# The layer norm's residual of a two-layer scan network: added by GpSimd, or by an accumulating DMA; norm and features centred in place

## The chip, the cores and the metric

The kernel runs on one core of a Trainium2 chip. A core has a matrix engine (PE, with its weight loads PEld), a vector engine (DVE), an activation engine (ACT), a general engine (POOL, or GpSimd) and a queue engine that only issues DMAs (SP). Each works through its own queue in order and waits for semaphores of the others. The metric is the device time of one execution in microseconds (us); the median of three runs is used.

## The reference, cut to what matters

The input x is 2 x 256 x 64 x 64, taken as 2 batches of 4096 tokens of 256 channels. Layer 0 is a group norm and one selective state-space scan. Layer 1 normalises each token, adds a forward and a backward scan of a second normalisation of it, and then a mixture of eight experts:

```python
x = x + _L0_conv_ref(_gn(x), ...)
t = _to_tokens(x)
t = t + _L1_attn_ref(_ln_t(t), ...)
t = t + _L1_ffn_ref(_ln_t(t), ...)

def _core(x, ln_gamma, ln_beta, fp, bp):       # called by _L1_attn_ref with x = _ln_t(t)
    xn = (x - mu) / jnp.sqrt(var + 1e-05) * ln_gamma + ln_beta
    y_fwd = _mamba(xn, *fp)
    y_bwd = jnp.flip(_mamba(jnp.flip(xn, 1), *bp), 1)
    return y_fwd + y_bwd + x
```

So layer 1's stream becomes t + ln(t) + y_fwd + y_bwd, where ln(t) is the norm before it is normalised again. The sum t + ln(t) is what the change touches. Everything is float32.

## The kernel before, in words

**Tiles and jobs.** A chunk is 512 tokens (T); a tile of the stream is 128 partitions x 2 halves of the channels x 512 (512 KB). Each batch has three jobs: layer 0 (256 inner channels, nj = 2), the forward scan of layer 1 (512, nj = 4) and the flipped one (nj = 4). A job does its 8 chunks in order; a chunk of a job is a *step* i, 48 in all. The stream t lives in DRAM (`t_dram`, one tensor per batch).

**The scan.** A step consists of nj x 4 *quads*. For a quad, POOL makes bq = rxdt x bc (line 737, 128x2048), ACT two halves of the decays da (line 747, into PSUM), DVE scans each half (line 773) and multiplies with C (line 782); for three quads of eight, and one half quad of sixteen, POOL does that multiplication (line 798). PE sums over the states (line 806). ACT also adds the carried state to the first element of bq (line 758) ahead of a half quad's decays.

**Order.** A *slot* is half a quad; step i starts at slot `starts[i]`, a forward or flipped step has 32 slots and one of layer 0 has 16. Everything beside the scan is put by hand at a slot and a queue with `sl.put(slot, queue, fn)`, relative to the start s0 of its step, and `in_order()` fixes each engine's queue in that order. In a slot, ACT first makes the decays of the next slot and then what was put there; DVE scans, then does what was put; POOL does its quads and then what was put. Matrix products of the experts fill free places: `experts()` chooses slots from counts of products, activations and PSUM banks that each part has registered with `sl.count`.

**The norm of a forward step** (`norm`): at slot -48 SP loads x from `t_dram` (line 370); PE takes the mean (line 389); DVE centres x into a tile cen (line 395); ACT squares (line 399); PE takes the variance (line 404); ACT makes the roots; DVE divides into nx (line 414), which is ln(t), and scales cen for the second normalisation (line 415), both at slot -39 (late is 1 slot more in batch 0). At the same slot POOL adds x and nx (line 418). At -35 ACT writes gamma and beta's result over nx (line 422; -38 for the first chunk), and at -34 SP stores nx for the flipped job (line 428) and x back to `t_dram` (line 429). For the first chunk of a job all is 6 slots later.

**The end of a step** (`finish`): SP loads the stream into xr (line 829) 10 slots before the end of a forward or flipped step; PE projects the gated scan and adds xr (lines 836, 838) at 16 and 18 slots after the end (7 and 8 in layer 0); ACT copies the result back into xr (line 853); SP stores it to `t_dram` two slots after the second projection (line 854). For a flipped step `features` then makes the normalised features that the experts read: mean, centring by DVE into a tile fcen one slot after that store (line 871), square (line 876), variance, division (line 886) and a store to `nf_dram` (line 891). Tiles x, xr, and cen with fcen have one buffer each; nx has two.

**The last stage** (from line 1141) does the remaining experts and the gate, and is no part of the change.

Of the kernel before, what the change touches and what calls it, by code (L numbers as in the profile page):

```python
# [42 lines left out]
F32 = mybir.dt.float32  # L43
AF = mybir.ActivationFunctionType
ALU = mybir.AluOpType
AX = mybir.AxisListType

P = 128
NB, C, L = 2, 256, 4096
KC = C // P  # L50
T = 512
NCH = L // T
# [19 lines left out]
SLOTS = {  # L72
    2: dict(xs=(-23, -22), conv=(-20,), dbc=-16, dt=(-14, -13), z=(-10, -9), out=(7, 8)),
    4: dict(
        xs=(-31, -30, -24, -23), conv=(-26, -21), dbc=-17, dt=(-15, -13, -11, -9), z=(-6, -5, -3, -2),
        out=(16, 18),
    ),
}
AHEAD = 3
# [55 lines left out]
def hybrid_kernel(ctx: ExitStack, tc: tile.TileContext, a: dict, out: bass.AP):  # L135
    nc = tc.nc
# [32 lines left out]
    t_dram = [drp.tile([P, KC, L], F32, name=f"t_dram{b}") for b in range(NB)]  # L169
# [12 lines left out]
    def rsqrt(dst, src, eps, scale=1.0):  # L182
        nc.scalar.activation(dst, src, AF.Ln, bias=eps, scale=scale)
        nc.scalar.activation(dst, dst, AF.Exp, scale=-0.5)

    def over_channels(t):
        return t.rearrange("p (o t) -> p o t", o=1).to_broadcast([P, KC, T])


    with ExitStack() as st:  # L190
        wp = st.enter_context(tc.tile_pool(name="wp", bufs=1))
        wk = st.enter_context(tc.tile_pool(name="wk", bufs=1))
# [20 lines left out]
        sl = Slots()  # L213
# [130 lines left out]
        steps = [(job, c) for job in jobs for c in range(NCH)]  # L344
        starts = [sum(8 * job.nj for job, _ in steps[:i]) for i in range(len(steps) + 1)]
# [3 lines left out]
        def norm(i):  # L349

            (job, c), ck, tag, s0 = steps[i], cks[i], tags[i], starts[i]
            s = job.cols(c)
            b = job.batch
            if job is jobs[AHEAD]:
                return

            def alloc():
                ck["nx"] = wk.tile([P, KC, T], F32, tag="nx", name=f"nx_{tag}", bufs=2)

            if job.flip:  # L360
                def load():
                    alloc()
                    nc.sync.dma_start(ck["nx"], n2_dram[b][:, NCH - 1 - c, :, :])
                sl.put(s0 - 44, "sp", load)
                return

            def load_x():
                ck["x"] = wk.tile([P, KC, T], F32, tag="x", name=f"x_{tag}")
                src = t_dram[b] if job.layer else a["x"][b].rearrange("(k p) l -> p k l", p=P)
                nc.sync.dma_start(ck["x"], src[:, :, s])  # L370

            if job.layer == 0:
                def scale():
                    alloc()
                    for k in range(KC):
                        nc.scalar.activation(
                            ck["nx"][:, k, :], ck["x"][:, k, :], AF.Identity,
                            bias=job.gb[:, k : k + 1], scale=job.gs[:, k : k + 1],
                        )
                sl.put(s0 - 32, "sp", load_x)  # L380
                sl.put(s0 - 25, "act", scale)
                return

            def mean():
                ck["ps"] = psp.tile([P, T], F32, tag="ps", name=f"mean_{tag}")
                for k in range(KC):
                    nc.tensor.matmul(
                        ck["ps"], mean_w, ck["x"][:, k, :], start=(k == 0), stop=(k == KC - 1)  # L390
                    )

            def centre():
                ck["cen"] = wk.tile([P, KC, T], F32, tag="cen", name=f"cen_{tag}")
                nc.vector.tensor_tensor(ck["cen"], ck["x"], over_channels(ck["ps"]), ALU.subtract)

            def square():
                alloc()
                nc.scalar.activation(ck["nx"], ck["cen"], AF.Square)

            def variance():
                ck["var"] = psp.tile([P, T], F32, tag="ps", name=f"var_{tag}")
                for k in range(KC):
                    nc.tensor.matmul(
                        ck["var"], mean_w, ck["nx"][:, k, :], start=(k == 0), stop=(k == KC - 1)
                    )

            def roots():
                ck["r1"] = psp.tile([P, T], F32, tag="ps", name=f"r1_{tag}")
                rsqrt(ck["r1"], ck["var"], eps5)  # L410
                rsqrt(ck["var"], ck["var"], eps10, scale=1.0 + 1e-5)

            def divide():
                nc.vector.tensor_tensor(ck["nx"], ck["cen"], over_channels(ck["r1"]), ALU.mult)  # L414
                nc.vector.tensor_tensor(ck["cen"], ck["cen"], over_channels(ck["var"]), ALU.mult)

            def add():
                nc.gpsimd.tensor_tensor(ck["x"], ck["x"], ck["nx"], ALU.add)

            def affine():  # L420
                for k in range(KC):
                    nc.scalar.activation(
                        ck["nx"][:, k, :], ck["cen"][:, k, :], AF.Identity,
                        bias=lngb[:, 1, k : k + 1], scale=lngb[:, 0, k : k + 1],
                    )

            def store():
                nc.sync.dma_start(n2_dram[b][:, c, :, :], ck["nx"])
                nc.sync.dma_start(t_dram[b][:, :, s], ck["x"])

            late = 1 if NCH < i < 2 * NCH else 0
            for d, queue, fn in (
                (-48, "sp", load_x), (-44, "pe", mean), (-43, "dve", centre), (-42, "act", square),
                (late - 41, "pe", variance), (late - 40, "act", roots), (late - 39, "dve", divide), (late - 39, "pool", add),
                (-35 if c else -38, "act", affine), (-34, "sp", store),
            ):

                sl.put(s0 + d + (6 if c == 0 else 0), queue, fn)
            s0 += 6 if c == 0 else 0
            sl.count(s0 - 44, 2, 0, (1,))  # L440
            sl.count(s0 - 43, 0, 1)
            sl.count(s0 - 41, 2, 4, (2,))
            sl.count(s0 - 40, 0, 0, (1,))
            sl.count(s0 - (36 if c else 39), 0, 2.3)
# [376 lines left out]
        def finish(i):  # L821
            (job, c), ck, tag = steps[i], cks[i], tags[i]
            s, b = job.cols(c), job.batch
            v = {}

            def load():
                v["x"] = wk.tile([P, KC, T], F32, tag="xr", name=f"xr_{tag}")
                src = t_dram[b] if job.layer else a["x"][b].rearrange("(k p) l -> p k l", p=P)
                nc.sync.dma_start(v["x"], src[:, :, s])

            def over_time(m):
                return v["x"][:, m, ::-1] if job.flip else v["x"][:, m, :]

            def project(m):
                v[m] = psp.tile([P, T], F32, tag="ps", name=f"o_{tag}_{m}")
                nc.tensor.matmul(v[m], ident, over_time(m), start=True, stop=False)
                for j in range(job.nj):
                    nc.tensor.matmul(  # L838
                        v[m], job.w["out"][:, j, m * P : (m + 1) * P], ck["sz", j],
                        start=False, stop=(j == job.nj - 1),  # L840
                    )

            s0 = starts[i + 1]

            before = steps[i - 1][0].nj if i else 0
            sl.put(max(s0 - (10 if job.nj == 4 else 5), starts[i] + (21 if before == 4 else 0)), "sp", load)

            slots = SLOTS[job.nj]["out"] if i + 1 < len(steps) else (3, 4)
            for slot in slots:
                sl.count(s0 + slot, 1 + job.nj, 1, (1,))  # L850
            for m, slot in enumerate(slots):
                sl.put(s0 + slot, "pe", lambda m=m: project(m))
                sl.put(s0 + slot + 1, "act", lambda m=m: nc.scalar.copy(over_time(m), v[m]))
            sl.put(s0 + slot + 2, "sp", lambda: nc.sync.dma_start(t_dram[b][:, :, s], v["x"]))
            if job.flip and i + 1 < len(steps):
                features(b, NCH - 1 - c, v, s0 + slot + 2)

        def features(b, c, v, s0):
# [8 lines left out]
                    )  # L867

            def centre():
                v["cen"] = wk.tile([P, KC, T], F32, tag="cen", name=f"fcen_{b}{c}")  # L870
                nc.vector.tensor_tensor(v["cen"], v["x"], over_channels(v["ps"]), ALU.subtract)

            def square():
# [217 lines left out]
        for g in range(nq):  # L1091
            i, jp, n = quads[g]
# [47 lines left out]
    with ExitStack() as st:  # L1140
# [5 lines left out]
        n, x, y, acc, wts, wb, lt, w_dram = {}, {}, {}, {}, {}, {}, {}, {}  # L1146
# [329 lines left out]
```

## Time and profile before

| | |
|---|---|
| median of 3 runs | 5069.14 us (5067.45 to 5076.32) |
| the profiled execution | 5072.22 us, its span 5070.5 us |
| busy, share of the span | PE 84%, DVE 90%, ACT 71%, POOL 87% |
| scan stage | first scan at 61.6 us, last one at 4475.2 us |
| add of line 418 on POOL | 16 times, 2.36 us (median) |
| line 737 on POOL | 640 times, 4.54 us |
| line 773 on DVE | scans of 128x1024, 2.34 us each |
| DMA | 873 MB, 172 GB/s over the span |

How to read it: the page of one profiled execution gives busy times and the span in 40 slices, as tenths; lines are named by engine, line, operation, out<-in and shape, with the number of instances. The view by windows gives the busy time of each engine between two times. The view of waits lists who waited for whom (total, times, longest, in us). In the timeline a line gives start and length in us, and in brackets the idle time of the engine just before and what ended it. "DMA to landing" is the time from an issue until its semaphore tells that the data have arrived.

### The profile page before, as it was taken

To read this page: it belongs to the slowest core of one execution; us is meant where nothing else is said; L and a number is where in the kernel's file an instruction comes from. 1 tells how busy PE (TensorE), PEld (TensorE's weight loads), DVE (VectorE), ACT (ScalarE), POOL (GpSimd) and SP (SyncE) were. 2 spreads that over 40 slices of the span, in tenths; PEclk is the share of its full clock that TensorE was granted. 3 is DMA by queue.
4 is the path that set the end of the run, shared out by engine and by line. 5 is a ranking of instruction groups with operands and counts; after the bars stand their busy time and mean duration, and the time that the engine had idled before them with its cause. 6 is when DMAs were issued, how large, how long until landed. Compare 5 with 4: busy or idle time off the path is not lost. (4 is left out here: it accounts for less than half of the span.)

```text
span 5070.5 us, 47370 instructions
## 1 busy us (share of the span) xinstructions
PE 4247.6 (84%) x14920; PEld 1478.8 (29%) x14920; DVE 4581.4 (90%) x3096; ACT 3609.1 (71%) x7319; POOL 4409.8 (87%) x1442
## 2 busy tenths in 40 slices
PE   5667787787777899989999888898868999888997
PEld 1222222222222333333333333333222333334443
DVE  6998999999999999999999999999999999946635
ACT  5677777777776877877787888878777788742231
POOL 5998999999999999999999999999999999931110
PEclk8788889899888999999999999999889999999998
DMA  5455444444444444457675555544444554544533
GB/s 189 155 172 180 160 159 160 146 155 155 170 167 155 162 171 165 160 198 246 233 243 185 175 184 178 188 161 172 140 160 167 175 177 158 175 168 175 199 112 137
DMA packets 333947, 873.15 MB, mean 172 GB/s; under 512 B 36408, under 2 KB 111936, under 8 KB 291712
## 3 DMA queue, kind: packets, MB, share of 16 engines
q1 hardware_dynamic: 329408, 842.73, 48.4%
q0 software_dynamic: 4288, 27.40, 1.4%
q8 instruction: 118, 1.93, 0.2%
q14 instruction: 133, 1.09, 0.1%
HBM read 671.17 MB, written 198.84 MB: 172 GB/s over the span
## 5 line engine op out<-in xcount | busy, mean ns | idle before, releaser
L737 POOL TENSOR_TENSOR bq<-rxdt,bc 128x2048 f32<-128x2048 f32 x640 | 2892.7, 4541 | 17.3 <-DMA rxdt<-xdtd 8.3
L747 ACT ACTIVATE da<-rdt,w_a 128x512 f32<-128x512 f32 x2560 | 1757.3, 686 | 110.3 <-DVE bq L773 63.9
L773 DVE TENSOR_TENSOR_SCAN da<-da,h_state,bq 128x1024 f32<-128x1024 f32 x664 | 1558.0, 2346 | 55.3 <-ACT da L747 44.7
L798 POOL TENSOR_TENSOR bq<-bq,bc 128x2048 f32<-128x2048 f32 (+1 forms) x280 | 1180.0, 4214 | 22.5
L773 DVE TENSOR_TENSOR_SCAN bq<-da,h_state,bq 128x1024 f32<-128x1024 f32 x456 | 1059.5, 2339 | 23.7 <-ACT da L747 23.7
L806 PE MATMUL y<-bq,stack 128*32 128x512 f32 x5120 | 741.9, 665 | 275.3 <-POOL bq L798 251.5
L782 DVE TENSOR_TENSOR bq<-da,bc 128x1024 f32<-128x1024 f32 x760 | 926.3, 1219 | 15.7
L989 PE MATMUL e<-eh,ew 128*128 128x512 f32 x1376 | 671.6, 622 | 63.9 <-DMA ew<-in_Wo 17.0
L792 ACT COPY h_state<-da 128x2 f32<-128x2 f32 x759 | 119.3, 157 | 634.1 <-DVE bq L782 632.3
L758 ACT ACTIVATE bq<-h_state,bq,a 128x1 f32<-128x1 f32 x1120 | 430.2, 384 | 2.7 <-POOL bq L737 2.0
L989 PEld LDWEIGHTS e<-eh,ew 128*128 128x128 f32 x1376 | 250.7, 194 | 475.9 <-issue 239.9
L806 PEld LDWEIGHTS y<-bq,stack 128*32 128x32 f32 x5120 | 140.1, 116 | 820.2 <-POOL bq L798 359.7
L450 PE MATMUL z<-nx,w_in 128*128 128x512 f32 x640 | 329.1, 643 | 58.1 <-DVE nx L414 21.2
L523 PE MATMUL conv<-xs,w_conv 64*64 64x512 f32 x2560 | 330.1, 602 | 23.5 <-ACT xs L507 21.3
L989 PE MATMUL e<-en,ew 128*128 128x512 f32 x688 | 323.8, 604 | 22.9 <-DVE fcen L886 15.8
L450 PE MATMUL xs<-nx,w_in 128*128 128x512 f32 x640 | 317.3, 625 | 21.1 <-DVE xc L536 7.9
L1287 ACT ACTIVATE h<-hp,of,sc 128x512 f32<-128x512 f32 x168 | 130.4, 777 | 252.2 <-PE hp L1283 235.6
L838 PE MATMUL o<-sz,w_out 128*128 128x512 f32 x640 | 298.3, 605 | 0.0
L1000 ACT ACTIVATE eh<-e,of,sc 128x512 f32<-128x512 f32 x344 | 259.3, 767 | 44.1 <-PE e L989 43.9
L590 POOL TENSOR_TENSOR xdt<-sp,xc 128x512 f32<-128x512 f32 x160 | 203.3, 1275 | 46.0 <-DVE sp L586 45.8
L773 DVE TENSOR_TENSOR_SCAN da<-da,bq 128x1024 f32<-128x1024 f32 x96 | 219.4, 2285 | 3.8 <-ACT da L747 2.2
L1248 POOL TENSOR_TENSOR x<-x,bi 128x1024 f32<-128x1024 f32 x16 | 37.2, 2338 | 188.8 <-DMA x<-t_dram 108.0
(141 smaller groups left out, 4924.1 us busy)
## 6 DMA issues: line engine op xcount, KB each, us to landing
rxdt<-xdtd SPq DMA_DIRECT2D x160, 1024.0 KB, 6.6
rdt<-dtd SPq DMA_DIRECT2D x160, 1024.0 KB, 6.5
bc<-bcd SPq DMA_DIRECT2D x384, 256.0 KB, 3.2
ew<-in_W SPq DMA_DIRECT2D x172, 256.0 KB, 5.0
u<-u SPq DMA_DIRECT2D x86, 512.0 KB, 4.3
u<-eu SPq DMA_DIRECT2D x82, 512.0 KB, 4.3
dtd<-sp SPq DMA_DIRECT2D x160, 256.0 KB, 3.5
xdtd<-xdt SPq DMA_DIRECT2D x160, 256.0 KB, 3.4
```

Of the source, the lines that this page charges most:

```text
L450: nc.tensor.matmul(ps, job.matrices["in", half][:, k, j * P : (j + 1) * P], rhs, start=(k == 0), stop=(k == KC - 1),)
L523: nc.tensor.matmul(v[r][64 * col : 64 * col + 64, :], job.matrices["conv"][rows, 2 * jp + j, k, :], ck["xs", jp][rows, j, k : k + T] if k ...
L737: nc.gpsimd.tensor_tensor(bq[g], ck["rxdt", j], over_groups(ck["bc", 0, sg]), ALU.mult)
L747: nc.scalar.activation(da[g, h][:, k, :], cks[i]["rdt", j][:, q, :], AF.Exp, scale=steps[i][0].w["a"][:, j, q * SG + sg : q * SG + sg + 1],)
L758: nc.scalar.activation(bq[g][:, q, 0:1], job.h[:, j, sg, q : q + 1], AF.Identity, scale=cks[i]["a0", j][:, h, sg : sg + 1], bias=bq[g][:, ...
L773: nc.vector.tensor_tensor_scan(b if on_pool(g, h) else d, d, b, job.h[:, j, sg, 2 * h : 2 * h + 1] if c else 0.0, ALU.mult, ALU.add,)
L782: nc.vector.tensor_tensor(bq[g][:, two, :], d, cks[i]["bc", 1, sg].rearrange("p (o t) -> p o t", o=1).to_broadcast([P, 2, T]), ALU.mult,)
L798: nc.gpsimd.tensor_tensor(b, b, cks[i]["bc", 1, sg].rearrange("p (o t) -> p o t", o=1).to_broadcast([P, groups, T]), ALU.mult,)
L806: nc.tensor.matmul(y[i, j][q * CG : (q + 1) * CG, :], stack, bq[g][:, q, :], start=False, stop=(sg == SG - 1),)
L838: nc.tensor.matmul(v[m], job.w["out"][:, j, m * P : (m + 1) * P], ck["sz", j], start=False, stop=(j == job.nj - 1),)
L989: nc.tensor.matmul(ps, ew[l][:, k, m * P : (m + 1) * P], key[x][:, k, :], start=(k == 0), stop=(k == KC - 1),)
L1000: nc.scalar.activation(key[dst][:, m, :], key["ps", l, m], AF.Relu, bias=of[:, l, e, m : m + 1], scale=sc[:, l, e, m : m + 1],)
```

## The change

In `norm`, x is centred in place, so cen is gone. The sum t + ln(t) is no longer made in SBUF by POOL and stored by SP: POOL issues, at the same slot, a DMA that adds nx to the rows of `t_dram`. Line 429's store goes. ACT's affine step, which writes over nx, waits for that DMA instead of for the add. In `features`, the centring writes xr itself, which is then squared, divided and stored from there; fcen is gone. Because xr is now held until the feature store, the load of xr in flipped steps moves from 10 slots before the step's end to 2, and the last flipped step of batch 0 (i = 23), whose successor is a short layer-0 step, projects at slots 7 and 8 instead of 16 and 18. In the instruction order of the built program the 16 adds are replaced by 16 DMA issues at the same places of POOL's queue, SP has 16 issues fewer, and PE's, ACT's and DVE's queues hold as many instructions as before, moved only around step 23 to 33; as many expert products (1032) stand in the scan stage.

```diff
             def centre():
-                ck["cen"] = wk.tile([P, KC, T], F32, tag="cen", name=f"cen_{tag}")
-                nc.vector.tensor_tensor(ck["cen"], ck["x"], over_channels(ck["ps"]), ALU.subtract)
+                nc.vector.tensor_tensor(ck["x"], ck["x"], over_channels(ck["ps"]), ALU.subtract)
 
             def square():
                 alloc()
-                nc.scalar.activation(ck["nx"], ck["cen"], AF.Square)
+                nc.scalar.activation(ck["nx"], ck["x"], AF.Square)
...
             def divide():
-                nc.vector.tensor_tensor(ck["nx"], ck["cen"], over_channels(ck["r1"]), ALU.mult)
-                nc.vector.tensor_tensor(ck["cen"], ck["cen"], over_channels(ck["var"]), ALU.mult)
+                nc.vector.tensor_tensor(ck["nx"], ck["x"], over_channels(ck["r1"]), ALU.mult)
+                nc.vector.tensor_tensor(ck["x"], ck["x"], over_channels(ck["var"]), ALU.mult)
 
             def add():
-                nc.gpsimd.tensor_tensor(ck["x"], ck["x"], ck["nx"], ALU.add)
+                nc.gpsimd.dma_start(t_dram[b][:, :, s], ck["nx"], accum_op=ALU.add)
 
             def affine():
                 for k in range(KC):
                     nc.scalar.activation(
-                        ck["nx"][:, k, :], ck["cen"][:, k, :], AF.Identity,
+                        ck["nx"][:, k, :], ck["x"][:, k, :], AF.Identity,
...
             def store():
                 nc.sync.dma_start(n2_dram[b][:, c, :, :], ck["nx"])
-                nc.sync.dma_start(t_dram[b][:, :, s], ck["x"])
...
-            sl.put(max(s0 - (10 if job.nj == 4 else 5), starts[i] + (21 if before == 4 else 0)), "sp", load)
-
-            slots = SLOTS[job.nj]["out"] if i + 1 < len(steps) else (3, 4)
+            sl.put(max(s0 - (2 if job.flip else 10 if job.nj == 4 else 5), starts[i] + (21 if before == 4 else 0)), "sp", load)
+
+            slots = SLOTS[2 if i == AHEAD * NCH - 1 else job.nj]["out"] if i + 1 < len(steps) else (3, 4)
...
             def centre():
-                v["cen"] = wk.tile([P, KC, T], F32, tag="cen", name=f"fcen_{b}{c}")
+                v["cen"] = v["x"]
                 nc.vector.tensor_tensor(v["cen"], v["x"], over_channels(v["ps"]), ALU.subtract)
```

## The prediction

> **What bounds the kernel now.** First the page: busy tenths of the two fullest engines over 40 slices of the span.
>
> ```profile
> DVE  6998999999999999999999999999999999946635
> POOL 5998999999999999999999999999999999931110
> ```
>
> Up to slice 35 both read 9: the scan stage (61.6 to 4475 us) is what the change touches, and its last stage is mixed. A share cannot tell which of two full engines binds, so I cut the stage into steps (one chunk of one scan; its ends are the starts of the scans of line 773) and ask for the busy time of each engine in three of them: a forward step of batch 0, one of batch 1, and a flipped step.
>
> ```profile
> core 0: us, PE busy (x) PEld busy (x) DVE busy (x) ACT busy (x) POOL busy (x), PEclk, DMA share, GB/s
> 751.20:863.80 112.60, 89.13 (x357) 28.22 (x356) 111.08 (x77) 88.15 (x184) 112.04 (x39) 0.89 0.45 159
> 2948.60:3058.80 110.20, 97.93 (x365) 34.28 (x364) 108.06 (x72) 89.92 (x185) 109.64 (x36) 0.97 0.55 182
> 4043.40:4152.40 109.00, 99.34 (x365) 34.08 (x364) 106.69 (x70) 87.63 (x182) 107.58 (x35) 0.97 0.52 179
> ```
>
> In the forward steps POOL is idle 0.56 us of 112.6 and of 110.2; DVE 1.5 and 2.1. The waits, asked for one stretch of each batch, settle it: POOL has no wait at all from 637.9 to 1314.2 us, and one of 1.2 us from 2730 to 3500. DVE's in the first and, below, in the second stretch:
>
> ```profile
> DVE da L773 <- ACT da L747: 8.7, 8, 2.8
> DVE xc L536 <- ACT thx L532: 1.0, 5, 0.2
> ```
> ```profile
> DVE da L773 <- ACT da L747: 9.4, 11, 3.5
> DVE da L773 <- issue: 2.5, 7, 0.5
> DVE xc L536 <- ACT thx L532: 2.4, 7, 0.6
> ```
>
> So in the forward steps POOL binds, and DVE follows about 1.5 us a step behind being the bound itself: 10 us of waits in the first stretch and 14.7 in the second (0.4 more in a smaller row). A gain on POOL ends there. The residual add is in those steps. Its neighbourhood, by the timeline (start, length):
>
> ```profile
> 729.99 1.21 DVE L414 TENSOR_TENSOR nx<-cen,r 128x1024 f32<-128x1024 f32 x1
> 739.62 2.36 POOL L418 TENSOR_TENSOR x<-x,nx 128x1024 f32<-128x1024 f32 x1
> 742.01 1.52 ACT L422 ACTIVATE nx<-cen,lngb 128x512 f32<-128x512 f32 x2 [0.66 <-POOL x L418]
> ```
> ```profile
> 3034.12 1.21 DVE L414 TENSOR_TENSOR nx<-cen,r 128x1024 f32<-128x1024 f32 x1
> 3041.14 2.36 POOL L418 TENSOR_TENSOR x<-x,nx 128x1024 f32<-128x1024 f32 x1
> 3049.13 1.50 ACT L422 ACTIVATE nx<-cen,lngb 128x512 f32<-128x512 f32 x2
> ```
>
> Two things are to be seen. POOL comes to its add 8.4 us (batch 0) and 5.8 us (batch 1) after nx is ready: that lag is how far POOL is behind DVE. And ACT overwrites nx in the affine step as soon as the add is done, in batch 0 already after a wait.
>
> **What the Trainium skill says.** "DMA: Bandwidth & Descriptors", section "SWDGE vs HWDGE vs iDMA": accumulating during a DMA is only possible from GpSimd. So the issue stays on the engine that binds; no run here shows an accumulating DMA. The same page, "Anatomy of one DMA — SWDGE (gpsimd) path", prices a plain one at 2.0 us + bytes/436 GB/s, an estimate of 3.2 us for 512 KB; the four stores that POOL issues here (u<-eu) land in 2.9 to 3.3 us, which agrees. Nothing prices the accumulation. "SBUF — State Buffer", section "SBUF: two separate sides": a VectorE instruction with two SBUF inputs and a GpSimd one that reads SBUF lock each other out. In the scan stage DVE's large operations have one operand in PSUM, and line 737 on POOL lies between 4500 and 4582 ns over 640 instances: no lock shows, so less POOL work doesn't make DVE faster.
>
> **The change part by part.** The sum is made against the profiled execution: 5072.2 us, of which the span is 5070.5; the median of the runs is 5069.1, 3.1 less.
>
> *The add leaves POOL's arithmetic.* 16 adds of 2.36 us. In each place stands, by the instruction order of the built program, one DMA issue of 256 rows of 512. The nearest row is the load of that form that POOL issues in the last stage:
>
> ```profile
> L1168 POOL DMA_DIRECT2D n<-t_dram x1: 721/721/721, 4820.9 to 4820.9; - x1
> ```
>
> 0.72 us, the next POOL instruction being unslowed after such issues (nm at 4572.71: 2.36). Bounds: 0.53 (plain form) to 2.4 (as long as the add; then nothing is won). I take 0.72: 1.64 us saved each, 26 in all. Of the 16, 12 lie where POOL has no wait (six a batch): 19.7 us. The other four lie at the ends of layer-0 steps; the two first ones of a batch even wait for DVE (1.77 and 0.71 us), so I count those four at nothing. DVE then binds: in batch 0 relief of 9.8 meets 10 us of DVE waits, some of which are ACT's own crowding, in batch 1 14.7. I take off 2 us in each: **-15.7**.
>
> *The affine step now waits for the landing.* Line 422 rewrites nx, which the DMA reads; ACT, in order, holds behind it the decays (line 747) that DVE scans next, so what ACT waits there DVE waits. The time to landing, D, is the unknown. From below: the plain store of the same rows, 3.1. From above: the one load from t_dram on POOL's queue, 13.4, which stood behind others. In between: the removed store 5.2, a load from t_dram 5.1, and 1.7 for the smallest transfer, which is mostly fixed cost.
>
> ```profile
> t_dram<-xr SPq DMA_DIRECT2D x48, 512.0 KB, 3.1
> xr<-t_dram SPq DMA_DIRECT2D x32, 512.0 KB, 5.1
> t_dram<-x SPq DMA_DIRECT2D x16, 512.0 KB, 5.2
> bcd<-dbc_rows SPq DMA_DIRECT2D x48, 64.0 KB, 1.7
> n<-t_dram POOLq DMA_DIRECT2D x1, 512.0 KB, 13.4
> ```
>
> The removed store itself landed in 3.6 to 4.3 us in batch 0 (seven landings are in the trace) and in 5.2 to 9.4 in batch 1, where expert weights and activations keep the queues fuller. An accumulation reads the target and then writes it: 3.6 + (5.1 - 1.7) = 7.0 for batch 0; for batch 1, where the store was 8 with another one just ahead of it, I take 9. Against it stands the time from the add's start to the affine in the 16 chunks of the timeline: 6.0 and 5.3, six times 2.4, then 6.6, 10.1, 7.9 and five times 8 to 9.2. The first two of batch 0 wait 1.0 and 1.7, the first of batch 1 2.4, the second not; the last six of batch 1 wait about 1 until POOL is that much earlier. In the six of batch 0, ACT is ready about 10.3 us after the start of the division, 9.1 after its end, so nothing is waited if POOL's lag is under 9.1 - 7 = 2.1. It is 8 now; but a wait of ACT holds DVE alone and lets POOL catch up, and POOL is 1.64 us lighter. The lag thus sinks to about 2, in two or three chunks, and the waits on the way are paid for by the lag. Exposed: 1.0 + 1.7 + 2.4 and 1 for leftovers: **+6**.
>
> *Features centred in place.* Line 871 now writes xr, which the store of line 854 reads. DVE has the scans behind it. Store and centring of one chunk:
>
> ```profile
> 1820.17 0.55 SPq L854 DMA_DIRECT2D t_dram<-xr  x1
> 1824.58 1.19 DVE L871 TENSOR_TENSOR fcen<-xr,fmean 128x1024 f32<-128x1024 f32 x1
> ```
>
> The store lands 3.1 us after its start, 1.3 before DVE comes. Of the 12 of 15 with a landing in the trace, one lands 0.2 late. The cover is thin: a store at 5.2 would cost 0.8 each, 12 in all. I take **+1**; below nothing isn't possible.
>
> *At nothing:* the norm centred in place (same instruction; x is free sooner than by its store); 16 SP issues fewer (0.55 us each; SP isn't the bound); another 8.4 MB read (1% of the traffic at a DMA share near 0.5); the flipped load of xr 8 slots later: it now stands behind the feature store of line 891 on SP and waits for its landing, with loads of bc and rdt queued behind it, but that store is three slots (about 10 us) old by then, and the product that reads xr comes 18 slots on, about 60 us; the last flipped chunk of batch 0 projected 9 slots earlier, which shifts expert products in the layer-0 steps of batch 1 (within 3 us either way). The number of early experts and the last stage are unchanged.
>
> Sum: -15.7 + 6 + 1 = -8.7; 5072.2 - 8.7 = 5063.5, less 3.1: **5060**.
>
> **Rivals.** (a) *All relief counts*: D near 5, and DVE's waits were all POOL's: -26: 5043. For it: POOL never waits; against: DVE's margin of 1.5 us a step. (b) *Gain hidden*: D 2 us longer than I take, 9 and 11. The early chunks wait 3.0 + 3.7 + 4.4 = 11, the six none more, but the lag must be near 0, which leaves 2 us of new waits; -15.7 + 11 + 2 + 1 + 1 = -1: 5068. (c) *Slower: ACT bound to the landing.* From D = 9.1 on (batch 0) even a POOL without lag lands too late for the six chunks, and every further us is paid six times. At 11 and 13: the early chunks 5.0 + 5.7 + 6.4 = 17; the six 2.0 each less the 0.9 us that DVE has left in such a step, 7, and no relief there; batch 1 -8 + 3; features 1: +20: 5089. For it: ACT stands ready at the affine step now, and a read and a write in one transfer aren't in this trace. Against: plain transfers of 512 KB land in about 3 to 5 us at the median.
>
> **How the numbers follow.** Main case 0.45 (own range 5050 to 5068, 0.13 of it above 5059), (a) 0.10, (b) 0.17, (c) 0.28. The bound of 0.2%, about what a measurement of this kernel tells from no change, is 10 us. Faster 0.32 + 0.10 = 0.42; same 0.13 + 0.17 = 0.30; slower 0.28. Range 5044 to 5090: it leaves out half of (a) and the worst half of (c).
>
> **What would show it.** Right: POOL's issues near 0.7 us; steps from 751 to 1200 us at about 111.7 instead of 112.6, from 2950 to 3280 at about 108.7 instead of 110.2; landings near 7 and 9; the affine step waiting in early chunks alone; the distance from the division to the issue down to about 2 us in batch 0. Wrong: issues over 2 us (no relief), landings over 9 (ACT waits in every forward step of batch 0), or DVE waits for the store at the feature centring in most of 15 chunks.

## The result, and the profile after

| | before | after |
|---|---|---|
| median, runs | 5074.13 us (5067.45 to 5079.63, 5 runs) | 5092.04 us (5090.04 to 5097.29, 5 runs) |
| ratio | | 1.0040, 95% interval 1.0025 to 1.0054 |
| profiled execution, its span | 5072.22 us, 5070.5 us | 5090.04 us, 5088.3 us |

The changed kernel is slower by 0.4%. The forecast was 5060 us, faster; the time lies just above its range's upper end of 5090. Line numbers of after are one or two below those of before (add 418 is 417, affine 422 is 421, bq 737 is 735, decays 747 are 745, scan 773 is 771, multiplications 782 and 798 are 780 and 796; the copies of the state that POOL makes ahead of its multiplications, 797, are 795).

The page's slices are nearly the same, so the busy shares tell nothing:

```profile
DVE  6998999999999999999989999999999999946635
POOL 5998999999999999999999999999999999931110
```

Cut by jobs (start of a job's first scan to the start of the next one's, us), the place shows. The first row is before; the others are differences to it. The experiments' rows are used further on. Each row is one profiled execution, and executions of one kernel differ by up to 14 us in all (before, beside E11: 5063.6 to 5077.5), so a difference of 1 to 3 us in one job is not read as an effect by itself. Single steps repeat far better: the fourth to sixth of the forward job of batch 0 take 112.65 to 112.69 us each in before, E2, E3, E5, E9 and E11.

| kernel | up to the first scan | layer 0, b. 0 | forward, b. 0 | flipped, b. 0 | layer 0, b. 1 | forward, b. 1 | flipped, b. 1 | after the scans |
|---|---|---|---|---|---|---|---|---|
| before | 61.6 | 469.7 | 897.0 | 871.4 | 430.7 | 878.5 | 868.7 | 593.0 |
| after | -1.0 | +2.5 | **+27.4** | -4.7 | +2.0 | -6.1 | -4.0 | +1.8 |
| E1 own tile | +0.5 | -0.1 | +3.4 | -3.1 | +3.8 | -6.4 | -2.5 | +1.4 |
| E2 load alone | -1.0 | -0.4 | +0.6 | -4.0 | +2.7 | -2.2 | -2.0 | +1.0 |
| E3 features half | -0.1 | +0.1 | +0.9 | -4.3 | +0.8 | -1.0 | -4.1 | +0.4 |
| E4 norm half | -0.7 | +1.1 | +32.8 | -0.2 | -0.5 | -6.6 | +1.7 | +1.2 |
| E5 affine step later | +0.5 | +1.0 | +1.2 | -4.7 | +2.9 | -6.3 | -1.2 | +2.2 |
| E6 no add at all | -0.5 | +1.2 | +7.5 | -4.0 | +0.2 | -6.6 | -1.8 | +1.2 |
| E7 roots later, own tile | -0.8 | +4.6 | +36.9 | -4.5 | +0.4 | -6.2 | -2.0 | +1.9 |
| E8 roots later, POOL's add | 0.0 | +5.2 | +36.5 | -4.0 | +0.1 | -0.2 | -4.0 | +0.2 |
| E9 DMA in batch 1 alone | +0.7 | +0.3 | +0.8 | -4.1 | +3.5 | -6.4 | -2.0 | +1.6 |
| E10 plain store | -0.3 | +0.4 | +24.2 | -4.0 | +0.3 | -6.7 | -1.9 | +1.0 |
| E11 issue earlier | -1.3 | +0.9 | +0.8 | -4.6 | +5.4 | -6.2 | -3.7 | +2.1 |
| E12 reload later | +0.1 | -0.4 | +15.5 | -4.8 | +5.2 | -5.9 | -4.1 | +0.6 |

One job loses 27.4 us, the flipped jobs and the forward job of batch 1 gain 14.8, the rest is +5.3. The view by windows for the same three steps as before (length, then busy time and count of PE, PEld, DVE, ACT and POOL, clock, DMA share, GB/s):

```profile
759.53:876.43 116.90, 90.32 (x356) 27.10 (x355) 111.47 (x77) 88.14 (x184) 110.71 (x38) 0.89 0.47 154
2952.40:3062.10 109.70, 100.27 (x365) 34.70 (x364) 108.03 (x71) 89.93 (x185) 108.96 (x36) 0.95 0.57 182
4038.40:4146.10 107.70, 99.07 (x367) 34.50 (x366) 106.65 (x70) 87.36 (x182) 107.14 (x35) 0.98 0.51 179
```

The forward step of batch 0 is 4.3 us longer than before with the same DVE work (111.47 against 111.08) and less on POOL (its 1.1 us of issuing isn't counted as busy): neither binds there now. Both wait, as the view of waits of after in the second to sixth forward steps of batch 0 (643.1 to 1230.5 us) shows:

```profile
ACT nx L421 <- DMA t_dram<-nx: 28.8, 5, 6.1
POOL h_state L795 <- DVE bq L771: 22.5, 15, 2.4
DVE sz L614 <- ACT thz L611: 16.7, 5, 3.7
DVE da L771 <- ACT da L745: 7.1, 10, 0.9
```

ACT waits for the landing in each of these five steps, 5.2 to 6.1 us; DVE then waits for ACT, and POOL, which had no wait here before, for DVE. Of the 16 issues (line 417) the profile says, duration in ns and landing in us:

```profile
L417 POOL DMA_DIRECT2D t_dram<-nx x16: 1037/1070/1284, 403.5 to 3393.3; - x16
DMA to landing us min/median/max: 5.7/6.3/8.5
```

One such chunk in the timeline of after:

```profile
852.35 1.21 DVE L413 TENSOR_TENSOR nx<-x,r 128x1024 f32<-128x1024 f32 x1
854.04 2.36 POOL L796 TENSOR_TENSOR bq<-bq,bc 128x1024 f32<-128x1024 f32 x1
856.35 4.55 POOL L735 TENSOR_TENSOR bq<-rxdt,bc 128x2048 f32<-128x2048 f32 x1
860.83 1.10 POOL L417 DMA_DIRECT2D t_dram<-nx  x1
868.08 1.52 ACT L421 ACTIVATE nx<-x,lngb 128x512 f32<-128x512 f32 x2 [5.19 <-DMA t_dram<-nx]
870.12 0.69 DVE L614 SCALAR_TENSOR_TENSOR sz<-thz,z 128x512 f32<-128x512 f32 x1 [2.77 <-ACT thz L611]
```

nx is ready at 853.56. POOL does 6.9 us of its own work before it issues, 7.27 us after; the data land 7.23 us later; ACT, free at 862.89, has stood still for 5.19 us. Behind its affine stand thz and the decays, for which DVE waits. In the six forward steps the distance from division to issue is 8.19, 7.30, 7.27, 7.27, 7.27, 7.26: after the first step it does not shrink at all, though ACT waits each time. The landing takes 6.37, 7.50, 7.23, 8.03, 8.15, 8.09 us there, and 5.7 to 6.2 in the last six of batch 1. In these six chunks of batch 1 the issue comes 4.4 to 5.0 us after the division and ACT's turn 8.1 to 9.4 us after the issue: no wait.

POOL's queue of before in the same chunk, where the division ends at 844.46 us:

```profile
845.44 2.35 POOL L798 TENSOR_TENSOR bq<-bq,bc 128x1024 f32<-128x1024 f32 x1
847.75 4.54 POOL L737 TENSOR_TENSOR bq<-rxdt,bc 128x2048 f32<-128x2048 f32 x1
852.23 2.36 POOL L418 TENSOR_TENSOR x<-x,nx 128x1024 f32<-128x1024 f32 x1
```

The same two instructions stand ahead of the add: of the 7.8 us between division and add they take 6.8. In the six steps of before that distance is 7.6 to 8.4 us.

In the forward job of batch 1 (2730 to 3500 us) POOL's waits went from 1.2 us up to 3.5, and DVE's from 14.7 down to 8.4. Two rows of that view of after:

```profile
POOL h_state L795 <- DVE bq L771: 3.5, 6, 1.1
DVE da L771 <- ACT da L745: 1.8, 5, 0.5
```

Before, the second of these rows was 9.4 (this job lies 26 us later in after; in a window moved along with it, 2756 to 3526, the row is 3.8). That fits a DVE that waited for POOL's bq by way of ACT, whose carry (line 758) comes ahead of the decays and reads bq, so POOL's relief reaches it; no run tests this path by itself.

### The profile page after: what moved, and what is told of

The parts are those of the page before. It is cut to its first block, busy times and chain, and to the rows that moved or that the text cites. A ratio compares the mean times of both kernels' runs of the same rounds, so it can differ in the third digit from the quotient of the medians.

```text
span 5088.3 us, 47382 instructions
## 1 busy us (share of the span) xinstructions
PE 4263.0 (84%) x14920; PEld 1480.6 (29%) x14920; DVE 4582.9 (90%) x3096; ACT 3609.7 (71%) x7319; POOL 4390.9 (86%) x1442
## 5 line engine op out<-in xcount | busy, mean ns | idle before, releaser
L780 DVE TENSOR_TENSOR bq<-da,bc 128x1024 f32<-128x1024 f32 x760 | 927.1, 1220 | 15.7
L521 PE MATMUL conv<-xs,w_conv 64*64 64x512 f32 x2560 | 345.3, 617 | 37.7 <-ACT xs L505 35.4
L811 PE MATMUL y<-xc,w_d 128*128 128x512 f32 x320 | 185.5, 663 | 24.2 <-DVE sz L817 24.2
```

The costliest lines, as they stand in the source:

```text
L521: nc.tensor.matmul(v[r][64 * col : 64 * col + 64, :], job.matrices["conv"][rows, 2 * jp + j, k, :], ck["xs", jp][rows, j, k : k + T] if k ...
L780: nc.vector.tensor_tensor(bq[g][:, two, :], d, cks[i]["bc", 1, sg].rearrange("p (o t) -> p o t", o=1).to_broadcast([P, 2, T]), ALU.mult,)
```

## The experiments

The theory after the result: the shared tile makes a ring of POOL's issue, the landing, ACT's affine step and DVE's next work, and of the add's relief only that in batch 1 is worth anything. The rivals: that the accumulating DMA itself disturbs other transfers; that the features' half costs; that POOL's relief is worth its 2.36 us wherever it falls. Each ratio is to executions of before made beside the run (medians 5072.1 to 5074.5 us).

**E1, a tile of its own for the DMA's source** (against after). ACT's affine no longer overwrites what the DMA reads.

```diff
-                nc.vector.tensor_tensor(ck["nx"], ck["x"], over_channels(ck["r1"]), ALU.mult)
+                ck["ln"] = wk.tile([P, KC, T], F32, tag="cen", name=f"ln_{tag}")
+                nc.vector.tensor_tensor(ck["ln"], ck["x"], over_channels(ck["r1"]), ALU.mult)
...
-                nc.gpsimd.dma_start(t_dram[b][:, :, s], ck["nx"], accum_op=ALU.add)
+                nc.gpsimd.dma_start(t_dram[b][:, :, s], ck["ln"], accum_op=ALU.add)
```

> The changed kernel, but the normalised tile that the accumulating DMA reads is one of its own (the 4 KB per partition that cen has given up), so that ACT's affine step writes nx without waiting for the landing. Theory A (the loss is ACT's wait for the landing, which DVE and then POOL pay too): the affine step waits for nothing, the forward job of batch 0 falls from 924 to about 895 us, and the kernel comes to about 13 us under the kernel before (0.997). Rival B (the loss is the accumulating DMA itself, its issue on POOL or its traffic, and ACT's wait only shows it): the forward job stays near 920 and the kernel about 15 us over the kernel before (1.003).

Measured: 5066.46 us (5061.03 to 5069.44), ratio to before 0.9984 (0.9976 to 0.9992). The forward job of batch 0 falls from +27.4 to +3.4 (a little under before was expected). The transfers are the same, in that job they land 4.8 to 8.8 us after the affine step has begun, and nothing waits for that. So the loss is the wait on the shared tile and not a disturbance by the DMA.

**E2, the later load of xr alone** (against before).

```diff
-            sl.put(max(s0 - (10 if job.nj == 4 else 5), starts[i] + (21 if before == 4 else 0)), "sp", load)
+            sl.put(max(s0 - (2 if job.flip else 10 if job.nj == 4 else 5), starts[i] + (21 if before == 4 else 0)), "sp", load)
```

> The kernel before with one line of the change: the load of xr in flipped steps 8 slots later (10 to 2 before the step's end). Theory C (the flipped jobs became shorter because SP no longer stands at that load behind the feature centring, with the store of dt behind it, whose tile ACT needs): both flipped jobs shorten by 4 to 5 us each, the kernel by about 9 (0.998). Rival D (the gain of the flipped jobs is from centring in place, which frees the other tile): no change, within 2 us.

Measured: 5066.77 us (5063.39 to 5070.97), 0.9986 (0.9980 to 0.9993). An edit that the prediction costed at nothing gains as much as any other here, within the intervals; in the flipped jobs it is 4.0 and 2.0 us, where 4 to 5 each were expected. The view of waits of before, from 1535 to 2190 us, shows why:

```profile
SPq L829 <- DVE fcen L871: 9.7, 6, 2.5
ACT sp L581 <- DMA dtd<-sp: 12.8, 5, 2.8
DVE sp L586 <- ACT h_state L792: 7.1, 6, 1.6
```

xr has one buffer. SP came to its next load before DVE had read the last xr for the centring and stood there; behind it in SP's queue waited the store of dtd, which holds one of the three "th" buffers; ACT's softplus needed that buffer, and DVE the softplus. With the load eight slots later SP has no wait for fcen, DVE none for ACT at sp, and ACT's wait is 5.7 us, for POOL.

**E3, the whole features' half** (against before): E2's line, i = 23 projected earlier, and

```diff
-                v["cen"] = wk.tile([P, KC, T], F32, tag="cen", name=f"fcen_{b}{c}")
+                v["cen"] = v["x"]
```

> The kernel before with the whole features half of the change: centred in place, the load of xr later, the last flipped chunk of batch 0 projected earlier; the norm and POOL's add as before. Theory C: as in the run with the load alone, about -9 us (0.998), the centring in place costing under 2. Rival (in place costs DVE a wait for the store at each of 15 centrings): at least 5 us longer than with the load alone.

Measured: 5066.73 us, 0.9988 (0.9981 to 0.9994), like E2. Centring in place adds nothing beyond.

**E4, the norm's half alone** (after without E3's lines).

> The kernel before with the norm half of the change alone: x centred in place and the accumulating DMA, features as before. Theory A: all the loss is here; the forward job of batch 0 is 27 us longer, that of batch 1 4 to 6 shorter, the flipped jobs as before, and the kernel about 25 us over the kernel before (1.005). Rival (the halves hurt each other, say by their traffic or the order of loads): under 18 us over.

Measured: 5102.23 us (5100.92 to 5103.85), 1.0056 (1.0043 to 1.0069); +32.8 in the forward job of batch 0. The whole loss is in this half, and the features' half had been hiding about 10 us of it.

**E5, the affine step and nx's store one slot later in batch 0** (against after).

```diff
-                (-35 if c else -38, "act", affine), (-34, "sp", store),
+                (late - 35 if c else -38, "act", affine), (late - 34, "sp", store),
```

> The changed kernel with one shared tile as it is, but in the forward job of batch 0 the affine step and its store one slot later (about 4 us). Theory A: the affine step waits 5.2 to 6.1 us for the landing now, so about 1.5 to 2 are left in five of six chunks; the forward job of batch 0 falls from 27 us over the kernel before to about 8 over, and the kernel to about its time before (1.000). Rival B (the wait isn't the cause, only a sign of it): it stays 25 us over in that job and the kernel at 1.003 to 1.004.

Measured: 5073.35 us (5067.81 to 5078.45), 0.9998 (0.9990 to 1.0006). From 640 to 1200 us ACT still waits for the landing, 6.7 us in four waits of at most 2.1, and the forward job of batch 0 is +1.2, where +8 was expected. The profiled execution is the fastest of the 13, 5.5 us under the median, but the last three of these four steps take 112.67 us each, just as before. A wait of 2 us is covered, one of 5 to 6 is not.

**E6, no add at all** (E3 with the body of the add left out: the residual ln(t) is not added).

```diff
-                nc.gpsimd.tensor_tensor(ck["x"], ck["x"], ck["nx"], ALU.add)
+                pass
```

> The kernel before with the features half of the change, and POOL's add left out with nothing in its place: the residual ln(t) isn't added to the stream. It measures what 2.36 us less on POOL is worth in each norm. Theory E (in batch 0 DVE with ACT needs as long as POOL does, 112.6 us a step, by ACT's crowding at its softplus and roots, so relief of POOL is worth nothing there): the forward job of batch 0 within 3 us of 897, that of batch 1 about 6 shorter, the kernel at 0.9975. Rival F, as in the prediction (POOL binds, and DVE's waits are POOL's): the forward jobs 9 to 10 us shorter each, the kernel at 0.995 or below.

Measured: 5069.08 us, 0.9989 (0.9982 to 0.9996): the same as E3, which has the adds. 16 x 2.36 us off POOL are worth nothing measurable in the whole. By jobs, +7.5 in the forward job of batch 0, where theory E had at most 3 and the rival a gain, and -6.6 in that of batch 1, as theory E had it. In the former (640 to 1200 us) POOL now waits, and DVE waits more for thx (1.0 us in E3):

```profile
POOL h_state L797 <- DVE bq L773: 8.8, 9, 1.0
DVE xc L536 <- ACT thx L532: 5.1, 10, 1.8
```

DVE is bound there by itself and by ACT; what POOL is given it spends waiting. Why the steps become longer, 113.2 to 114.6 us instead of 112.7, stays open, so E6 is not a clean measure of the relief in batch 0; E11 below is the better one.

**E7 and E8, the roots, the division and the affine step one slot later in batch 0**, in E1 (E7) and in E3 (E8), to make the place less crowded.

```diff
-            late = 1 if NCH < i < 2 * NCH else 0
+            late = 2 if NCH < i < 2 * NCH else 0
...
-                (-35 if c else -38, "act", affine), (-34, "sp", store),
+                (late - 35 if c else -38, "act", affine), (late - 34, "sp", store),
```

> The changed kernel with the tile of its own, and in the forward job of batch 0 variance, roots, division, affine step and its store one or two slots later than in the kernel before, away from ACT's softplus. Theory E: DVE's wait of 0.9 us a step for a decay that ACT makes late goes, and as POOL is lighter now, the job falls from 900 to about 893 us and the kernel to about 0.997. Rival (the crowding only moves): 900 again.

> The kernel before with the features half of the change and the same later roots, the add still on POOL. Theory E: POOL's own work of 112.6 us a step now binds alone, so DVE's wait may go but the job stays at about 897, the kernel at 0.9988 as with the features half alone. Rival (POOL never bound, only DVE with ACT): the job falls by 5 us here too.

Measured: 5105.09 us, 1.0061 (1.0048 to 1.0073), and 5111.44 us, 1.0069 (1.0056 to 1.0082). Both missed, for a reason that has nothing to do with the add: at the new slot the roots fall behind the load of ACT's next function table. From 884 to 1121 us E8 has eight table loads of 1283 ns on lines 183 and 184 that E3 has not, four a step, 5.1 us; DVE waits 2.65 us and 1.88 us a step for the roots. On batch 0 they tell nothing of the question. But they are one more pair with and without POOL's add: 36.9 and 36.5 in the forward job of batch 0, -6.2 and -0.2 in that of batch 1.

**E9, the accumulating DMA in batch 1 alone** (E3; batch 0 keeps POOL's add and its store).

```diff
-                nc.gpsimd.tensor_tensor(ck["x"], ck["x"], ck["nx"], ALU.add)
+                if b:
+                    nc.gpsimd.dma_start(t_dram[b][:, :, s], ck["nx"], accum_op=ALU.add)
+                else:
+                    nc.gpsimd.tensor_tensor(ck["x"], ck["x"], ck["nx"], ALU.add)
```

> The features' half of the change in both batches, and the accumulating DMA in batch 1 alone; batch 0 keeps POOL's add and the store of x. Theory: the relief of POOL is real in batch 1 (its forward job was 6 us shorter in each of the four kernels measured so far in which the add was off POOL, 1 to 2 in the two that kept it) and worth nothing in batch 0, so the forward job of batch 1 takes 872 us instead of 878, the one of batch 0 stays within 2 us of before, the flipped jobs keep their 4 each: 0.9976, 5062 us. Rival: what batch 1's forward job gains is given back in the steps after it, since SP, PE and the expert products set their times: 0.9987, as with the features alone.

Measured: 5066.26 us (5061.08 to 5068.15), 0.9984 (0.9977 to 0.9991). The forward jobs come out as the theory has them (+0.8 and -6.4), the total nearer to the rival: the layer-0 job of batch 1 is +3.5 and the last stage +1.6. Part of the relief is thus not seen at the end; with one profiled execution, whether those two are really longer stays open.

**E10, a plain store in the accumulation's place** (against after; ln(t) overwrites the stream, so the residual t is lost).

```diff
-                nc.gpsimd.dma_start(t_dram[b][:, :, s], ck["nx"], accum_op=ALU.add)
+                nc.gpsimd.dma_start(t_dram[b][:, :, s], ck["nx"])
```

> The changed kernel with the accumulation taken out of the DMA: POOL's transfer writes ln(t) over the stream instead of adding it, so the residual t is lost; queue, rows, tile and waits are the same. Theory: the long landing is the price of the accumulation, its read of the target ahead of the write: the landing falls from 8 to about 4 to 4.5 us in the forward steps of batch 0, ACT's wait there from 6 to about 2.3, and the forward job of batch 0 is 5 to 8 us longer than before instead of 27: ratio 0.999 to 1.000. Rival: the landing is long because of what else is in flight (the reload of rxdt, 1 MB, issued 2.5 us ahead): it stays at 7 us or over, the wait over 4.5, and the ratio at 1.003 to 1.004.

Measured: 5087.77 us (5082.29 to 5092.04), 1.0025 (1.0016 to 1.0035); +24.2 in the job. Of its 16 issues the profile says:

```profile
L417 POOL DMA_DIRECT2D t_dram<-nx x16: 642/666/846, 403.6 to 3388.4; - x16
DMA to landing us min/median/max: 3.1/4.2/7.4
```

Both theories were half right, and the total is nearer to the rival's. In the last six chunks of batch 1, where no 1 MB load has been issued ahead of them, the plain store lands in 3.1 us and the accumulating one in 5.7 to 6.2: accumulating costs about 3 us there. In the six of batch 0 the plain one takes 5.9 to 7.2 as well and ACT waits 3.9 to 5.4. There the 1 MB reload of rxdt has been issued 2.6 us ahead (at 855.88 us, landing at 863.46, the store in flight from 858.44 to 864.72).

**E11, the issue ahead of POOL's work in the same slot** (against after): emitted with DVE's division, it stands before the half multiplication and bq in POOL's queue.

```diff
-                (late - 41, "pe", variance), (late - 40, "act", roots), (late - 39, "dve", divide), (late - 39, "pool", add),
+                (late - 41, "pe", variance), (late - 40, "act", roots), (late - 39, "dve", divide), (late - 39, "dve", add),
```

> The changed kernel with the issue of the accumulating DMA put into POOL's queue straight after the division, ahead of the half multiplication and the bq that POOL has in the same slot in batch 0 (6.9 us of work), instead of behind them; the shared tile, the affine step and everything else stay. Theory: the 7.3 us from division to issue are those instructions of POOL and nothing else, so the distance falls to 0.5 us or less, the data land at about the time at which ACT comes (6 to 8 us after, ACT being ready 9.1 us after the division's end), ACT waits under 1 us in the six forward steps of batch 0, and that job loses its 27 us but for 0 to 3: 0.9985, 5066 us, the level of the copy of its own tile. Rival: POOL, reaching the issue before the division is done, stands there for DVE and is late with bq: the forward job of batch 0 stays 8 us or more over before, ratio 1.000 or above.

Measured: 5063.60 us (5058.07 to 5067.36), 0.9983 (0.9976 to 0.9991). The same chunk in E11's timeline:

```profile
843.73 1.21 DVE L413 TENSOR_TENSOR nx<-x,r 128x1024 f32<-128x1024 f32 x1
845.24 1.09 POOL L417 DMA_DIRECT2D t_dram<-nx  x1
846.62 2.34 POOL L796 TENSOR_TENSOR bq<-bq,bc 128x1024 f32<-128x1024 f32 x1
848.93 4.54 POOL L735 TENSOR_TENSOR bq<-rxdt,bc 128x2048 f32<-128x2048 f32 x1
854.20 1.50 ACT L421 ACTIVATE nx<-x,lngb 128x512 f32<-128x512 f32 x2
```

The issue comes 0.30 us after the division; the landing still takes 7.28 us, at 852.52, and ACT's turn is 1.7 us later: no bracket, no wait. The rival did not take place: in the last five of the six steps POOL stands for the division 0.05 us at most, and once, at the end of layer 0, 3.4 us. The job is +0.8, its later steps 112.65 us against 112.67 before. With tile, transfer and affine step as in after, the place of one instruction in POOL's queue decides over 27 us. This version is faster than both kernels. It is not faster than E3 beyond the noise (0.9988, 0.9981 to 0.9994), which has POOL's add: that the accumulating DMA gains anything of its own in the whole is not shown.

**E12, the reload of rxdt after the landing** (against after).

```diff
-                for key, off in (("xdt", (-10, -12)[j % 2]), ("dt", -9)):
+                for key, off in (("xdt", (-10, -10 if NCH <= i < 2 * NCH else -12)[j % 2]), ("dt", -9)):
```

> The changed kernel with one load moved: in the forward steps of batch 0 the reload of rxdt for the odd channel groups is issued two slots later, so that SP issues it behind the store of nx, and so after the accumulating DMA has landed; bq needs it some four slots later. Theory: in these steps the landing is 2 us longer than the 6.1 of batch 1 because the 1 MB reload is in flight beside it: the landing falls to about 6.1, ACT's wait from 6 to 4, and the forward job of batch 0 takes about 12 us less than in the changed kernel, some 15 more than before: ratio 1.0015. Rival: the landing is longer in batch 0 for another reason (the neighbouring loads of bc, the rows of its tensor): it stays near 8 us and the ratio at 1.004. In either case, were the reload too late for POOL, POOL would wait for rxdt, which the waits would show.

Measured: 5079.23 us (5074.59 to 5084.36), 1.0013 (1.0005 to 1.0021); +15.5 in the job. Of its issues:

```profile
  ACT nx L421: 26.0, 8
DMA to landing us min/median/max: 5.7/5.8/7.5
```

In the six steps the landing is now 5.7 to 5.8 us and ACT waits 3.7 us (4.9 in the first), as the theory had it. So the 27 us are two terms: 15.5 from an undisturbed accumulation issued 7.3 us late, 12 from the reload in flight beside it. The terms do not simply add up: with the reload in flight, leaving out the accumulation takes away only 3 of the 27 (E10).

## Why the prediction was wrong, step by step

**What bounds** ("in the forward steps POOL binds, and DVE follows about 1.5 us a step behind"). Right for batch 1, but by less than it says. Four of the six steps there go from 110.2 to 109.7 us, with 1.29 us less on POOL (after) as with 2.36 less (E6), so POOL held them by 0.5 us and not by DVE's 2.1. Most of the rest of the gain is one step, the sixth, from 112.6 to 108.7 (109.4 in E6), in which DVE had waited 3.5 us for a decay. In batch 0 the two rows, 112.04 and 111.08 of 112.60, were read as a bound and a follower. E11 and E6 show two bounds: neither 1.29 nor 2.36 us less on POOL shortens a step of 112.67. DVE's 1.5 us of gaps stay, 0.9 at a decay that ACT makes too late and the rest at thx and in gaps too small to be named; a lighter POOL does not take them away.

**The relief** (-15.7). The issue occupies POOL for 1.07 us and not 0.72, so 1.29 us are saved each and not 1.64. In batch 1 the job gains 6.1 (5.9 to 6.7 in the nine other kernels that have no add there; E2, E3 and E8, which keep it, gain 2.2, 1.0 and 0.2) against 7.9 forecast. In batch 0 the gain is nothing (E11: +0.8) against 7.9.

**The wait for the landing** (+6). This is the step that failed. "Nothing is waited if POOL's lag is under 9.1 - 7 = 2.1" is right, and so was the landing in batch 0 almost: 7 forecast, 6.4 to 8.2 measured, 7.2 in the chunk shown. (In batch 1 it was 9 forecast and 5.7 to 6.2 measured in the last six chunks, which changed nothing. The waits in the early chunks, 1.0, 1.7 and 2.4 forecast, came out as 0.3, 3.1 and 2.2.) What failed is the next sentence, "a wait of ACT holds DVE alone and lets POOL catch up ... The lag thus sinks to about 2". The lag was 8.2 us in the first step and 7.3 in the other five, and the waits are what the prediction's own formula gives for that lag: 7.27 + 7.23 - 9.1 = 5.4, measured 5.19. It was taken for arrears that could be worked off. All but a few tenths of a microsecond of it is in fact work that stands ahead of the issue in POOL's in-order queue, 2.36 + 4.55 us of the same slot, as it stood ahead of the add before. POOL can't get ahead of it, and it gains nothing while ACT waits, since it waits for DVE at the state copies (22.5 us), DVE for ACT, ACT for the DMA, and the DMA for POOL. E11 takes those two instructions away from in front of the issue, and wait and loss are gone. In batch 1 the add's slot is an odd one, in which POOL has only an xdt of 1.3 us ahead of it, besides what is left of a bq already begun, and ACT comes to the affine step 13.2 to 13.8 us after the division and not 9.

The waits of the six chunks of batch 0 were costed at nothing but a share of the 1 us for leftovers; they cost 27 us, of which the reload in flight is 12 (E12). That a large load shares the time of the landing was not looked for: the plain store of before was issued by SP later, behind ACT, when the reload was over or nearly so (in the chunk of the timeline of before it lands at 857.60 us, the store runs from 856.60 to 860.26).

**Features in place** (+1). 0: E3 and E2 agree.

**At nothing.** The later load of xr was costed only for what it now stands behind, not for what no longer stands behind it. It gains 2 to 4 us in a flipped job (E2, E3): the term that kept the loss at 18 us.

The sum as measured: forward jobs +27.4 and -6.1, flipped ones -4.7 and -4.0, the rest +5.3: +17.9 on the span. Rival (c), slower, took place. ACT is bound to the landing in every forward step of batch 0, as it has it, but at landings that it held to be harmless: it put its threshold at a landing of 9.1 us, for a lag of nothing; at a lag of 7.3 ACT waits from a landing of 1.8 on, and with the 2 us that E5 shows covered it costs from about 4; the accumulation alone takes 5.7. That its 5089 us lies so near to the measured time is luck, since it rests on landings of 11 and 13 us.

**Left open.** Why the layer-0 job of batch 1 varies by 0 to 5 us between kernels. Why E1's and E6's steps in batch 0 are 0.5 to 2 us longer than E11's (DVE waits for thx there) with the same or more relief. No run moves POOL's add itself ahead of the slot's work. No version gained in the forward job of batch 0.

## What to carry to other kernels

When a step waits for another engine, ask whether the distance is arrears, which can be worked off, or instructions that stand ahead of it in an in-order queue, which can't; list those instructions before assuming that a lag shrinks. A compute step turned into a DMA moves its end from the engine's queue to the landing, so issue it ahead of the engine's long work in that slot, and don't let the next in-order engine overwrite its source. Of a load moved later, cost also what had been standing behind it in the queue.

## What the runs showed of the hardware that was not expected

- An accumulating DMA of 512 KB into DRAM (256 rows of 512 float32) lands in 5.7 to 6.2 us when no 1 MB load has been issued ahead of it, where the same DMA without accumulation lands in 3.1 (E10 against after, same place and rows). The latter agrees with the estimate of 3.2 us from the Trainium skill, "DMA: Bandwidth & Descriptors", section "Anatomy of one DMA — SWDGE (gpsimd) path"; the former has no price there.
- A 1 MB load in flight lengthens both: 5.9 to 7.2 us the plain one, 6.4 to 8.2 the accumulating one. E12 shows it by moving the load. In five of E11's six steps a load of 512 KB and two stores of 256 KB are in flight instead, and the accumulation takes 7.0 to 7.6.
- POOL is held 1.07 us by an accumulating issue and 0.67 by a plain one (medians of 16). In the chunks where the next instruction is a small copy (14 of 16), it starts 0.62 us after the issue's start in both; after an accumulating issue it takes 0.61 to 0.68 us and not 0.2 (0.23 to 0.28 after a plain one).
